# The mean of a first layernorm taken off on TensorE: seven chunks of x are turned, multiplied by a centering matrix and read from PSUM

## The chip, the core and the metric

The kernel runs on one core of one Trainium2 chip. A core has five engines, each with its own queue that is worked in order: TensorE (PE, with its weight loads as PEld), VectorE (DVE), ScalarE (ACT), GpSimd (POOL) and SyncE (SP), and 16 DMA engines that the queues feed. The metric is device time in microseconds (us) of the whole program; lower is better.

## The reference

Two graph-network layers run over 6250 nodes with 64 features and 206250 edges (`src`, `dst`, sorted by `dst`), each behind a layernorm and a relu, and each added to its input:

```python
def _layernorm(x, axis=-1, eps=1e-05):
    m = jnp.mean(x, axis=axis, keepdims=True)
    v = jnp.var(x, axis=axis, keepdims=True)
    return (x - m) / jnp.sqrt(v + eps)
...
h = jnp.maximum(_layernorm(x, axis=-1), 0.0)
x = x + _L0_gnn_ref(h, edge_index, ...)   # twice: h + segment_sum(h[src], dst), then relu(. @ Wa + ba) @ Wb + bb
h = jnp.maximum(_layernorm(x, axis=-1), 0.0)
x = x + _L1_gnn_ref(h, edge_index, ...)   # mlp of messages, segment sum, mlp of both
```

The change is in the first of the two layernorms only, which works on the kernel's input `x`.

## The kernel before

**Layout.** Nodes are cut into NT = 49 tiles of P = 128 nodes. `xs` holds all of x in SBUF, 128 partitions (nodes of a tile) by 49 tiles by D = 64 features. Seven DMAs, four on SP's queue and three on ACT's, bring it in chunks of XT = 7 tiles, the last with its short tile by itself.

**What the program does.** The edge list becomes a dense count matrix A, 6250 by 6250 in bytes, one tile of 128 destination nodes at a time; the segment sums are then products with A on TensorE. The stages are:

1. A prologue. `search` finds where each pair of destination tiles begins in the sorted list, by counting samples of `dst` (ACT, `junk` L312) and then, in `search_block`, entries of a gathered block (`junk` L336). `fetch_blocks` and `fetch_edges` are indirect DMAs issued on POOL (L325, L350) that bring the block and then the edges (`d_win`, `s_win`). `slots`, `cast` and `turn` (DVE, ACT, PE and ACT) make rows `lkw` of indices out of the edges. `values(t)` runs seven times, for the chunks that begin at tile 0, 7, 14, ..., 42: it makes the normed values `h` of seven tiles (`norm`, DVE and ACT) and splits them into three bf16 parts in `hp` (`split`, PE and ACT).
2. A build loop over the 49 tiles. `build(t, ...)` has DVE make one-hot patterns (`there` L414, `high` L418, `low` L421), PE multiply them into counts (`cnt` L446, sixteen at a time), ACT copy the counts (L448), and SP store them to DRAM. Between the quarters of `build(t)`, PE takes the first segment sum of tile t-1 (`acc` L594), which needs `hp` of all 49 tiles.
3. Two sweeps that load A again and take the second and third segment sums (`acc` L771).

**The first layernorm.** `norm` takes the sum over the 64 features (DVE, L239), scales it to a mean (L240), subtracts it (`xm`, L242), squares on ACT (L244), sums the squares (DVE, L246), takes the root on ACT (L247), the reciprocal on DVE (L248), and makes `h` by one DVE instruction that clips at zero and scales (L249). `split` copies `h` to bf16 on ACT (L256), and twice has PE put `h` less the parts so far into PSUM (L259, fp32, two passes each; L261, bf16) and ACT copy the rest to bf16 (L262).

**The order of the work.** A scheduler orders each engine's instructions by their place in the program and by when it takes them to be ready; waits follow from the data and the buffers. `behind(a, b)` fixes the order of two instructions on one engine. The calls ahead of the build loop stand in this order: `search(0)`, `fetch_blocks(0)`, `search(1)`, `fetch_blocks(1)`, `values(0)`, `search_block(0, 0)`, `fetch_edges(0)`, `values(7)`, `slots(0)`, `cast(0)`, `search_block(1, ..)`, `fetch_edges(1)`, `turn(0, 0)`, `values(14)`, `search(2)`, `fetch_blocks(2)`, `values(21)`, `search(3)`, `fetch_blocks(3)`, `values(28)`, `search_block(2, ..)`, `fetch_edges(2)`. `values(35)` and `values(42)` follow the first `build`.

**PSUM.** Eight banks: pool `pacc` has two (the segment sums `acc`), `pmix` two (tag `mix`, through `bank(...)`: the sample product, the turned rows, the layers), and `pcnt` two buffers of two banks, tile `cnt`, which `split` and `build` share. In SBUF `xm` has two buffers for the seven chunks.

In what follows chunk k, for k = 0 to 6, is the one of `values(7 * k)`.

Of the kernel before, what the change touches and what calls it, by code (L numbers as in the profile page):

```python
# [32 lines left out]
FP = mybir.dt.float32  # L33
# [7 lines left out]
OP = mybir.AluOpType  # L41
AX = mybir.AxisListType

P = 128
N = 6250
E = 206250
D = 64
# [6 lines left out]
CH = 512  # L54
# [20 lines left out]
XT = 7  # L75
# [83 lines left out]
def fast(ctx: ExitStack, tc: tile.TileContext, x, src, dst, w, bad, out):  # L159

    nc = tc.nc
# [3 lines left out]
    pacc = ctx.enter_context(tc.tile_pool(name="f_pacc", bufs=2, space=bass.MemoryType.PSUM))  # L165
# [3 lines left out]
    work = building.enter_context(tc.tile_pool(name="f_work", bufs=2))  # L169
    once = building.enter_context(tc.tile_pool(name="f_once", bufs=1))  # L170
# [3 lines left out]
    def bank(name, dtype=FP):  # L174
        return pmix.tile([P, CH * 4 // mybir.dt.size(dtype)], dtype, tag="mix", name=name)
# [7 lines left out]
    xs = const.tile([P, NT, D], FP, name="xs")  # L183
# [18 lines left out]
    nc.gpsimd.iota(high2, pattern=[[1, H], [0, 2]], base=HB, channel_multiplier=0, allow_small_or_imprecise_dtypes=True)  # L202
    which = once.tile([P, NQ], FP, name="which")
    nc.gpsimd.iota(which, pattern=[[P, NQ]], base=0, channel_multiplier=1, allow_small_or_imprecise_dtypes=True)
    ones = const.tile([P, P], FP, name="ones")
    nc.vector.memset(ones, 1.0)
    parts2 = [once.tile([P, MOST, 3, P], BF, name=f"parts{i}") for i in range(2)]
# [9 lines left out]
    ps = bank("ps_smp")  # L217
# [6 lines left out]
    hp = once.tile([P, NT, HP], BF, name="hp")  # L224
# [10 lines left out]
    def norm(to, t, n):  # L235

        xt = xs[:, t:t + n, :]
        mean = work.tile([P, n], FP, name="mean", tag=f"mean{n}")
        begun = nc.vector.tensor_reduce(mean, xt, axis=AX.X, op=OP.add)  # L239
        nc.vector.tensor_scalar_mul(mean, mean, 1.0 / D)  # L240
        xm = work.tile([P, n, D], FP, name="xm", tag=f"xm{n}")
        centered = nc.vector.tensor_tensor(xm, xt, mean[:, :, None].to_broadcast([P, n, D]), op=OP.subtract)  # L242
        sq = work.tile([P, n, D], FP, name="sq", tag=f"sq{n}", bufs=1)
        squared = nc.scalar.activation(sq, xm, AF.Square)  # L244
        var = work.tile([P, n], FP, name="var", tag=f"var{n}")
        nc.vector.tensor_reduce(var, sq, axis=AX.X, op=OP.add)  # L246
        nc.scalar.activation(var, var, AF.Sqrt, bias=w.eps, scale=1.0 / D)  # L247
        nc.vector.reciprocal(var, var)  # L248
        nc.vector.scalar_tensor_tensor(to, xm, 0.0, var[:, :, None].to_broadcast([P, n, D]), op0=OP.max, op1=OP.mult)  # L249
        return begun, centered, squared  # L250

    def split(parts, h):

        parts = [parts[:, :, i * D:(i + 1) * D] for i in range(NP)]
        banks = pcnt.tile([P, 2, CH], FP, name="cnt")[:, :, :h.shape[1] * D]
        nc.scalar.copy(parts[0], h)  # L256
        for i in range(2):
            ps = banks[:, i].rearrange("p (t d) -> p t d", d=D)
            nc.tensor.matmul(ps, w.ident, h, start=True, stop=False)  # L259
            for k in range(i + 1):  # L260
                nc.tensor.matmul(ps, minus, parts[k], start=False, stop=(k == i))  # L261
            nc.scalar.copy(parts[i + 1], ps)  # L262
# [20 lines left out]
    def tiles_of(b):  # L283
        return range(starts[b], starts[b] + BATCHES[b]), slice(starts[b], starts[b] + BATCHES[b])
# [3 lines left out]
    def behind(op, other):  # L288

        tc.add_manual_dep(op.ins, other.ins.name,  # L290
                          mybir.DependencyInfo(mybir.DependencyClass.NoSync, mybir.DependencyReason.DATA),
                          reason="order on an engine")
        return op

    def follow(op, engine):

        if engine in counted:
            behind(op, counted[engine])
# [6 lines left out]
    def search(b, after=None):  # L305

        if b >= len(BATCHES):
            return
        each, qs = tiles_of(b)
        for q in each:  # L310
            junk = wins.tile([P, NB], BF, name="junk", bufs=1)
            op = nc.scalar.activation(junk, smp, AF.Sign, bias=below_node[:, q:q + 1], accum_out=sign1[:, q:q + 1])  # L312
            if after:
                behind(op, after)
            follow(op, "ACT")
        nc.vector.tensor_scalar(row[:, qs], sign1[:, qs], -0.5, NB / 2 - 1, op0=OP.mult, op1=OP.add)
        return op, nc.vector.tensor_scalar(base[:, qs], sign1[:, qs], -0.5 * BLK, (NB / 2 - 1) * BLK + BLK / 2,
                                           op0=OP.mult, op1=OP.add)
# [21 lines left out]
    def fetch_edges(b):  # L340

        if b >= len(BATCHES):
            return
        each, qs = tiles_of(b)
        nc.vector.scalar_tensor_tensor(off_f[:, qs], sign2[:, qs], -0.5, base[:, qs], op0=OP.mult, op1=OP.add)
        nc.vector.tensor_scalar(off[:, qs], off_f[:, qs], float(E - P), None, op0=OP.min)  # L346
        lists[b] = [wins.tile([P, MOST, P], I32, name=name)[:, :len(each), :] for name in ("d_win", "s_win")]
        for win, of in zip(lists[b], (dst, src)):
            for i, q in enumerate(each):
                nc.gpsimd.indirect_dma_start(  # L350
                    out=win[:, i, :], out_offset=None, in_=of.rearrange("(a o) -> a o", o=1),
                    in_offset=bass.IndirectOffsetOnAxis(ap=off[:, q:q + 1], axis=0))
# [3 lines left out]
    def slots(b):  # L356

        if b >= len(BATCHES):
            return
        each, qs = tiles_of(b)  # L360
        n = len(each)
        d, s = lists.pop(b)

        def temp(name, dtype=I32, tag=None):
            return wins.tile([P, MOST, P], dtype, name=name, tag=tag or name, bufs=1)[:, :n, :]

        parts = parts2[b % 2][:, :n]

        def first(op):
            follow(op, "DVE")  # L370

        pair = temp("pair")
        first(nc.vector.tensor_scalar(pair, d, 1, PITCH // 2 - 1, op0=OP.logical_shift_right, op1=OP.bitwise_and))
        pair = pair.bitcast(I16).rearrange("p q (a b) -> p q a b", b=2)
        mine = temp("mine", FP)
        for i, q in enumerate(each):
            nc.vector.tensor_scalar(mine[:, i, :], pair[:, i, :, 0], which[:, q:q + 1], None,
                                    op0=OP.is_equal, op1=OP.add, accum_out=number[:, q:q + 1])
        high = temp("high_i")
        first(nc.vector.tensor_scalar(high, s, 7, 63, op0=OP.logical_shift_right, op1=OP.bitwise_and))  # L380
        nc.vector.scalar_tensor_tensor(parts[:, :, 1, :], mine, float(HB), high, op0=OP.mult, op1=OP.add)
        word = temp("word")
        first(nc.vector.tensor_scalar(word, s, 2, W - 1, op0=OP.logical_shift_right, op1=OP.bitwise_and))
        place = temp("place", tag="high_i")
        first(nc.vector.tensor_scalar(place, s, 3, PLACE_BIT, op0=OP.bitwise_and, op1=OP.logical_shift_left))
        second = temp("second", tag="mine")
        first(nc.vector.tensor_scalar(second, d, 1, SECOND_BIT, op0=OP.bitwise_and, op1=OP.logical_shift_left))
        place, second = (t.bitcast(I16).rearrange("p q (a b) -> p q a b", b=2)[:, :, :, 0] for t in (place, second))
        nc.vector.scalar_tensor_tensor(parts[:, :, 2, :].bitcast(I16), place, ONE_BITS, second,
                                       op0=OP.bitwise_or, op1=OP.bitwise_or)  # L390
        words[b] = word
# [118 lines left out]
        halves(h2r[:, t:t + n], ps[:, :n * HID].rearrange("p (t f) -> p t f", f=HID))  # L510

    def values(t):
        h = work.tile([P, XT, D], FP, name="h")
        begun, centered, squared = norm(h, t, XT)
        if t <= XT:
            behind(begun, sampled)
            behind(begun, bounds)
            behind(squared, searched[0])
        if t == XT:
            behind(centered, searched[1])  # L520
        split(hp[:, t:t + XT], h)


# [26 lines left out]
    searched = search(0)  # L550
    fetch_blocks(0)
    search(1)
    fetch_blocks(1)
    values(0)
    search_block(0, 0)
    fetch_edges(0)
    values(XT)
    slots(0)
    cast(0)
    for i in range(2):  # L560
        op = search_block(1, i)
    fetch_edges(1)
    turn(0, 0)
    values(2 * XT)
    search(2, op)
    fetch_blocks(2)
    values(3 * XT)
# [81 lines left out]
    work = ctx.enter_context(tc.tile_pool(name="f_work2", bufs=2))  # L649
# [14 lines left out]
    ps = bank("ps_stats")  # L664
# [133 lines left out]
    t, n = GROUPS[-1]  # L798
    acc, going = sweep(lambda k: [h2r[:, k, i, :] for i in range(2)], True, 0, conv2, (0, 2, 5, 7, 9, 11), (0, 1, 4, 5, 6, 8), [])
    going.append([conv2(t, n, acc), [0, 2, 10, 14, 17, 20]])  # L800
    acc, _ = sweep(lambda k: [yr[:, k].rearrange("p i d -> p (i d)")], False, 3, conv3, (0, 4, 8, 11), None, going)
# [254 lines left out]
```

## Time and profile before

| what | value |
|---|---|
| median of 5 runs | 878.99 us (878.92 to 880.21) |
| profiled execution, device time | 878.99 us |
| its span, first to last instruction | 877.1 us |
| mean granted TensorE clock | 0.993 |
| busy, share of the span | PE 96%, PEld 83%, DVE 73%, ACT 64%, POOL 16% |
| L239, L242, L246, L249 (DVE, 128x448 f32), seven each | 620, 614, 609, 617 ns (medians) |
| L244 (ACT, 128x448 f32), seven | 561 ns (median) |
| moved by DMA | 133.58 MB |

The device time is the span and 1.9 us around it. The profile is one execution, taken by the hardware profiler. Busy time is counted by engine, and instructions of one engine may overlap a little, so a sum of durations can pass the time that they took. A wait is put down to whichever releaser came last by the profile. PEclk is the share of TensorE's full clock that was granted.

### The profile page before, as it was taken

Reading aid. Unit: us, or ns where it says so; the run is one execution under the profiler, and the core shown is the slowest. Engines: PE = TensorE matmul, PEld = TensorE weight load, DVE = VectorE, ACT = ScalarE, POOL = GpSimd, SP = SyncE. Lnnn points to the kernel's source line nnn. Section 1 sums busy time; section 2 is a strip of 40 time slices with the busy share of each in tenths; the row PEclk is TensorE's granted clock in tenths of the full one; section 3 lists DMA queues with packets and bytes.
Section 4 is the critical chain, followed back from the end, with each engine's and each line's share of the span. In section 5 each row is a group of like instructions: output and inputs, shape, how many; then the busy total and the mean of one; then the engine's idle time right before and its main releaser. Section 6 shows DMA issues by size and latency. Waiting matters only on the chain.

```text
span 877.1 us, 19654 instructions
## 1 busy us (share of the span) xinstructions
PE 844.0 (96%) x8178; PEld 724.3 (83%) x8178; DVE 637.3 (73%) x957; ACT 565.6 (64%) x761; POOL 137.3 (16%) x86
## 2 busy tenths in 40 slices
PE   3789999999999999999999999999999999999996
PEld 1479999999999999887888787888889887777785
DVE  5899999999999999645555555555456677767662
ACT  5767777677777666645555555555555689877763
POOL 3545654435432300000000000000000000000000
PEclk9899999999999999999999999999999999999998
DMA  6345555556544434634443444444434477777771
GB/s 148 103 123 159 175 147 152 153 150 176 158 144 143 140 112 142 213 112 132 127 123 123 125 121 124 124 121 123 133 93 133 152 250 247 231 238 226 233 215 49
DMA packets 148327, 133.58 MB, mean 152 GB/s; under 512 B 29988, under 2 KB 110500, under 8 KB 148228
## 3 DMA queue, kind: packets, MB, share of 16 engines
q1 hardware_dynamic: 141784, 121.19, 46.3%
q0 software_dynamic: 3600, 10.32, 4.2%
q8 instruction: 66, 1.08, 0.5%
q10 hardware_dynamic: 2844, 0.72, 0.4%
q14 instruction: 33, 0.27, 0.1%
HBM read 91.25 MB, written 40.94 MB: 151 GB/s over the span
## 4 chain that ended last, share of the span: by engine, by line
PE 85%; ACT 6%; DMA 4%; DVE 3%; issue 1%; SPq 0%; POOL 0%; ACTq 0%; DVEq 0%
PE acc L771 44%; PE acc L594 21%; PE cnt L446 8%; PE ps_t L459 6%; PE ps_y L468 3%; ACT ar L762 2%; DMA a<-A 2%; ACT a L448 1%; PE ps_g L509 1%; ACT t L461 1%; ACT junk L312 1%; DMA blk<-in_dst_dram,row 1%; DMA xs<-in_x_dram 1%; PE cnt L259 1%; DMA s_win<-in_src_dram,off 0%
## 5 line engine op out<-in xcount | busy, mean ns | idle before, releaser
L762 DVE CAST ar<-a 128x2048 fp32r<-128x2048 uint8 (+1 forms) x200 | 220.3, 1110 | 175.4 <-PE acc L771 153.5
L762 ACT CAST ar<-a 128x2048 fp32r<-128x2048 uint8 (+2 forms) x126 | 232.1, 1846 | 117.1 <-PE acc L771 101.7
L771 PE MATMUL acc<-ar,h2r 128*128 128x512 f32 (+2 forms) x1274 | 297.1, 387 | 0.0
L771 PEld LDWEIGHTS acc<-ar,h2r 128*128 128x128 f32 x1274 | 228.8, 189 | 49.8 <-issue 5.8
L594 PE MATMUL acc<-hp,a 128*128 128x193 bf16 x2352 | 232.1, 247 | 1.4 <-ACT a L448 0.6
L448 ACT ACTIVATE a<-cnt 128x784 int16<-128x784 f32 x196 | 161.0, 822 | 69.6 <-PE cnt L446 68.7
L594 PEld LDWEIGHTS <-a 128*128 128x128 fp8e4 x2352 | 191.6, 97 | 3.4 <-ACT a L448 2.4
L771 PE MATMUL acc<-ar,yr 128*128 128x512 f32 (+2 forms) x637 | 156.9, 398 | 0.0
L771 PEld LDWEIGHTS acc<-ar,yr 128*128 128x128 f32 x637 | 115.5, 189 | 32.5 <-issue 9.4
L446 PEld LDWEIGHTS <-low 128*128 128x128 fp8e4 x3136 | 107.4, 96 | 8.9 <-issue 8.4
L446 PE MATMUL cnt<-high,low 128*128 128x49 bf16 x3136 | 114.0, 186 | 0.5 <-ACT a L448 0.3
L421 DVE TENSOR_TENSOR low<-there,lkw 128x2048 int32<-128x2048 bf16 (+2 forms) x51 | 112.2, 2200 | 0.0
L418 DVE TENSOR_TENSOR high<-high,lkw 128x3136 bf16<-128x3136 bf16 (+2 forms) x51 | 87.8, 1721 | 5.2 <-PE cnt L446 5.2
L325 POOL DMA_INDIRECT blk<-in_dst_dram,row x25 | 57.6, 2303 | 87.5 <-DVE own L590 74.4
L414 DVE TENSOR_TENSOR there<-word,lkw 128x2048 bf16<-128x2048 bf16 (+2 forms) x51 | 59.1, 1176 | 0.4
L350 POOL DMA_INDIRECT s_win<-in_src_dram,off x25 | 46.1, 1843 | 7.6 <-issue 7.6
L350 POOL DMA_INDIRECT d_win<-in_dst_dram,off x25 | 31.4, 1257 | 61.9 <-DVE off L346 46.2
L259 PE MATMUL cnt<-h,ident 128*128 128x448 f32 x28 | 17.7, 735 | 13.0 <-DVE h L249 10.3
L461 ACT ACTIVATE t<-ps_t,d 128x512 f32<-128x512 f32 (+2 forms) x26 | 17.3, 664 | 11.6 <-PE ps_t L459 11.6
L461 ACT ACTIVATE t<-ps_t,c 128x512 f32<-128x512 f32 (+1 forms) x26 | 17.1, 662 | 11.3 <-PE ps_t L459 11.3
L259 PEld LDWEIGHTS cnt<-h,ident 128*128 128x128 f32 x28 | 5.4, 233 | 19.9 <-issue 9.0
L336 ACT ACTIVATE junk<-blk,below_node 128x550 bf16<-128x550 int32 x25 | 18.7, 749 | 3.3 <-DMA blk<-in_dst_dram,row 3.3
(123 smaller groups left out, 606.1 us busy)
## 6 DMA issues: line engine op xcount, KB each, us to landing
a<-A SPq DMA_DIRECT2D x276, 256.0 KB, 2.8
A<-a SPq DMA_DIRECT2D x49, 768.0 KB, 4.1
a<-A SPq DMA_DIRECT2D x24, 192.0 KB, 2.4
a<-A SPq DMA_DIRECT2D x22, 64.0 KB, 2.0
out_dram<-o SPq DMA_DIRECT2D x11, 128.0 KB, 2.9
A<-a SPq DMA_DIRECT2D x49, 16.0 KB, 4.7
xs<-in_x_dram ACTq DMA_DIRECT2D x3, 224.0 KB
xs<-in_x_dram SPq DMA_DIRECT2D x3, 224.0 KB, 6.9
```

Of the source, the lines that this page charges most:

```text
L325: nc.gpsimd.indirect_dma_start(out=blks[q], out_offset=None, in_=dst.rearrange("(r b) -> r b", b=BLK), in_offset=bass.IndirectOffsetOnAxis ...
L350: nc.gpsimd.indirect_dma_start(out=win[:, i, :], out_offset=None, in_=of.rearrange("(a o) -> a o", o=1), in_offset=bass.IndirectOffsetOnAx ...
L414: nc.vector.tensor_tensor(there, word2[:, None, :, :].to_broadcast(shape), of(0)[:, :, None, :].to_broadcast(shape), op=OP.is_equal)
L418: nc.vector.tensor_tensor(high, high2[:, None, :, :].to_broadcast(shape), of(1)[:, :, None, :].to_broadcast(shape), op=OP.is_equal)
L421: counted["DVE"] = nc.vector.tensor_tensor(low.rearrange("p (g i) w -> p g i w", i=2), there.rearrange("p g w i -> p g i w"), of(2)[:, :, ...
L446: counted["PE"] = nc.tensor.matmul(ps[:, b, j * H:(j + 1) * H], low[:, g, :], high[:, g // 2, :, g % 2], start=True, stop=True)
L448: counted["ACT"] = nc.scalar.activation(a[:, :, k:k + 2 * PG].rearrange("p h (b j) -> p h b j", b=2), ps[:, :, :PG * H].rearrange("p b (j ...
L459: placed(nc.tensor.matmul(ps[:, :n * P], wt, rhs, start=(i == 0), stop=(i == len(terms) - 1)))
L461: nc.scalar.activation(to, ps[:, :n * P], AF.Relu, bias=bias)
L594: nc.tensor.matmul(acc[:, t % 2, :], self.own if k == t else self.a[:, k, :], hp[:, k], start=(k == order[0]), stop=(k == t))
L762: widen(ar.rearrange(f"p k t b -> {order}"), a.rearrange(f"p t (k b) -> {order}", b=P))
L771: op = nc.tensor.matmul(acc[:, :cols], part, ar[:, k - k0].rearrange("p t b -> p (t b)")[:, :cols], start=first, stop=(k == H - 1 and i == ...
```

## The change

The sum, its scaling and the subtraction leave VectorE for the first layernorm. In their place, for each chunk of seven tiles, TensorE turns pairs of tiles (128 nodes by 2 x 64 features, to 128 features by 128 nodes) into a PSUM bank, four of them, the last pair overlapping the third by one tile. The bank is copied to SBUF, by VectorE for chunks 0 and 1 and by ScalarE for the other five. TensorE then multiplies each turned pair by `center`, a 128 x 128 matrix of two 64 x 64 blocks with the identity less 1/64 on each, which gives the nodes' rows back with their mean taken off, in a PSUM bank of the pool `pacc`. ScalarE's square and VectorE's last instruction read them there. The rest of `norm` becomes `scaled`, which both layernorms use; the second layernorm keeps the mean on VectorE. The norm of chunk 2 is called ahead of `slots(0)`, while its `split` stays where it was. The fixed orders change with it.

```diff
+    center = once.tile([P, P], FP, name="center")
+    nc.gpsimd.memset(center, 0.0)
+    for j in range(0, P, D):
+        nc.gpsimd.memset(center[j:j + D, j:j + D], -1.0 / D)
+    nc.vector.tensor_tensor(center, center, w.ident, op=OP.add)
...
-        centered = nc.vector.tensor_tensor(xm, xt, mean[:, :, None].to_broadcast([P, n, D]), op=OP.subtract)
+        nc.vector.tensor_tensor(xm, xt, mean[:, :, None].to_broadcast([P, n, D]), op=OP.subtract)
+        scaled(to, xm, n)
+
+    def scaled(to, xm, n):
...
     def values(t):
+
+        ps = bank("xt")
+        sides = [(min(j, XT - 2), j - min(j, XT - 2)) for j in range(0, XT, 2)]
+        for i, (j, _) in enumerate(sides):
+            nc.tensor.transpose(ps[:, i * P:(i + 1) * P], xs[:, t + j:t + j + 2, :].rearrange("p t d -> p (t d)"), w.ident)
+        xt = work.tile([P, CH], FP, name="xt", tag="t1")
+        begun = (nc.vector.tensor_copy if t <= XT else nc.scalar.copy)(xt, ps)
+        xm = pacc.tile([P, CH], FP, name="acc")
+        for i, (j, o) in enumerate(sides):
+            nc.tensor.matmul(xm[:, (j + o) * D:(j + 2) * D], xt[:, i * P:(i + 1) * P], center[:, o * D:], start=True, stop=True)
         h = work.tile([P, XT, D], FP, name="h")
-        begun, centered, squared = norm(h, t, XT)
+        squared = scaled(h, xm[:, :XT * D].rearrange("p (t d) -> p t d", d=D), XT)
         if t <= XT:
             behind(begun, sampled)
             behind(begun, bounds)
-            behind(squared, searched[0])
-        if t == XT:
-            behind(centered, searched[1])
+        else:
+            behind(begun, searched[0])
+        behind(squared, searched[0])
+        if t == 2 * XT:
+            return h
         split(hp[:, t:t + XT], h)
...
     values(XT)
+    h = values(2 * XT)
     slots(0)
...
     turn(0, 0)
-    values(2 * XT)
+    split(hp[:, 2 * XT:3 * XT], h)
     search(2, op)
```

More of the change, by code (lines that the diff above doesn't have):

```diff
@@ L238, in norm @@
         mean = work.tile([P, n], FP, name="mean", tag=f"mean{n}")
-        begun = nc.vector.tensor_reduce(mean, xt, axis=AX.X, op=OP.add)
+        nc.vector.tensor_reduce(mean, xt, axis=AX.X, op=OP.add)
         nc.vector.tensor_scalar_mul(mean, mean, 1.0 / D)
         xm = work.tile([P, n, D], FP, name="xm", tag=f"xm{n}")
-        centered = nc.vector.tensor_tensor(xm, xt, mean[:, :, None].to_broadcast([P, n, D]), op=OP.subtract)
+        nc.vector.tensor_tensor(xm, xt, mean[:, :, None].to_broadcast([P, n, D]), op=OP.subtract)
+        scaled(to, xm, n)
+    def scaled(to, xm, n):
         sq = work.tile([P, n, D], FP, name="sq", tag=f"sq{n}", bufs=1)
@@ L249, in norm @@
         nc.vector.scalar_tensor_tensor(to, xm, 0.0, var[:, :, None].to_broadcast([P, n, D]), op0=OP.max, op1=OP.mult)
-        return begun, centered, squared
+        return squared
     def split(parts, h):
```

## The prediction

> **What bounds the kernel now.** I read the page's slices first (tenths busy in 40 slices of 21.9 us):
>
> ```profile
> PE   3789999999999999999999999999999999999996
> ...
> DVE  5899999999999999645555555555456677767662
> ACT  5767777677777666645555555555555689877763
> ...
> PEclk9899999999999999999999999999999999999998
> ```
>
> PE is full from the fourth slice to the last but one, and only the first three show room. The change touches nothing after them, so it can win or lose only there. Next, busy time by stretch (PE, PEld, DVE, ACT, POOL, then clock, DMA share, GB/s):
>
> ```profile
> 17.00:27.00 10.00, 8.29 (x21) 3.07 (x21) 8.03 (x29) 9.06 (x26) 5.99 (x7) 1.00 0.25 63
> 27.00:37.00 10.00, 7.13 (x31) 3.02 (x29) 8.41 (x26) 6.12 (x14) 6.78 (x7) 0.74 0.43 133
> 47.00:57.00 10.00, 6.97 (x111) 4.97 (x109) 9.79 (x22) 5.84 (x11) 8.23 (x6) 1.00 0.18 52
> ...
> 100.00:150.00 50.00, 49.77 (x904) 48.18 (x902) 49.38 (x72) 36.59 (x66) 29.53 (x14) 1.00 0.57 167
> ```
>
> By 100 us PE lacks 0.23 us in 50. So the end moves by as much as PE reaches that state sooner or later, at about 56 us. Ahead of it nobody is full throughout: ACT comes nearest in 17 to 27, DVE in 47 to 57. Which wait ends last is read in the timeline (start, duration, engine, line, then idle time before it and its releaser):
>
> ```profile
> 26.94 0.68 DVE L421 TENSOR_TENSOR low<-there,lkw 128x512 int32<-128x512 bf16 x1
> ...
> 30.17 0.75 ACT L336 ACTIVATE junk<-blk,below_node 128x550 bf16<-128x550 int32 x1 [1.33 <-DMA blk<-in_dst_dram,row]
> ...
> 30.92 0.28 ACT L247 ACTIVATE var<-var,eps 128x7 f32<-128x7 f32 x1
> 31.24 0.20 DVE L248 RECIPROCAL var<-var 128x7 f32<-128x7 f32 x1 [1.03 <-ACT var L247]
> ...
> 32.30 1.86 PE L259 MATMUL cnt<-h,ident 128*128 128x448 f32 x2 [2.00 <-DVE h L249]
> ...
> 34.33 0.87 PE L446 MATMUL cnt<-high,low 128*128 128x49 bf16 x16
> ...
> 37.87 0.61 DVE L242 TENSOR_TENSOR xm<-xs,mean 128x448 f32<-128x448 f32 x1
> ...
> 39.51 0.20 DVE L248 RECIPROCAL var<-var 128x7 f32<-128x7 f32 x1 [1.04 <-ACT var L247]
> ...
> 49.73 0.99 PE L259 MATMUL cnt<-h,ident 128*128 128x448 f32 x2 [2.53 <-DVE h L249]
> ```
>
> The patterns for the first counts are there at 27.62, yet the counts start at 34.33: PE stands at the split of chunk 4, whose root sat on ACT behind a `junk` that waited for a gathered block. From 26.13 (first pattern) to 51.79 (`low` of tile 2) DVE idles only 1.03, 0.34, 0.21 and 1.04 us, 2.6 in all: it carries the path there, with PE's splits and ACT's roots between. At 47.2 PE waits 2.53 us for chunk 6's `h`.
>
> **The change, part by part.** Prices come from these rows (groups: busy us, mean ns; timeline: the next line's start gives the occupancy):
>
> ```profile
> L267 DVE TENSOR_TENSOR h2r<-ps_g,h2r 128x512 fp32r<-128x512 f32 x12 | 8.3, 691 | 2.9 <-ACT h2r L266 2.6
> L266 ACT CAST h2r<-ps_g 128x512 fp32r<-128x512 f32 x12 | 7.0, 585 | 2.1 <-PE ps_g L509 0.9
> ```
> ```profile
> 82.59 0.38 PE L484 MATMUL tf<-ident,r 128*128 128x128 f32 x2
> 82.81 0.58 PE L446 MATMUL cnt<-high,low 128*128 128x49 bf16 x16
> ...
> 133.15 1.06 PE L509 MATMUL ps_g<-w,t 128*128 128x128 f32 x8
> 134.04 0.58 PE L446 MATMUL cnt<-high,low 128*128 128x49 bf16 x16
> ```
>
> *VectorE.* Gone: seven L239 at 0.620 and seven L242 at 0.614, 8.6 us, and seven L240, which showed 0.04 to 0.20 each, about 0.5. New: two copies out of PSUM, at most 0.691 each (L267 reads a second operand too), 1.4 us. Net 7.7 us less. Most of that lies before 25 us, where DVE also waits for gathers: of the L239, L240 and L242 only the `xm` at 37.87 comes after 26.3.
>
> *ScalarE.* Five copies of 0.585 (L266, same shape) to 0.69 (L461, 512 wide), 2.9 to 3.4 us; I take 2.9. The square reads PSUM instead of SBUF: nothing (0.561 now; L262 reads 448 from PSUM in 0.537). In 27 to 57 ACT has 9.6 us idle or waiting, which hides the copies there. In 17 to 27 only 0.94 is free. A copy is also a wait put into ACT's queue: behind it stand the search's `junk`, the roots and the casts of `hp`, and for them wait POOL's gathers and PE.
>
> *TensorE.* Per chunk four transposes (0.22 for two, so 0.44) and four fp32 products in eight passes (0.89): 1.33 us, 9.3 for seven, at full clock. At the slow one L259 shows 0.93 against 0.51 a pass, so up to 2.4 a chunk. PE now idles 4.8 us between 8.68 and 13.46, which hides chunks 0 and 1, and again 2.0 before 32.30 and 4.2 from there to 56. Work on chunks 5 and 6 falls into that end at 2.7 us, and only what is left of the idle time pays for it. A chunk's `xm` comes 0.44 + 0.16 fill + 0.69 + 0.89 + 0.17 fill = 2.35 us after PE begins, against 1.9 from 7.87 to 9.76 now. No one waits for chunk 0 that early.
>
> *New buffer waits.* `xm` takes the two banks that the first segment sum uses. The first `acc` then needs chunk 5's `h` done; that ended at 41.34 and the first L594 began at 41.27, so the wait costs nothing unless chunk 5 falls back. The turned rows share two banks with the sample product and with `turn`: a late copy would hold up `turn(0, 0)` (24.48) behind it on PE.
>
> *The rest.* `center` costs POOL three memsets and DVE one 128x128 add (the casts L193 took 0.22), in POOL's idle time from 2.8 to 10.95 and DVE's from 1.1 to 5.76: nothing; without that cover, under 1 us. The earlier norm of chunk 2 moves DVE and ACT work ahead of `slots(0)`, past no DMA of its own.
>
> [...] PE ran at a granted 0.50 in 32 to 38 us after 2.0 us of idle; the two L259 pairs there took 1.86 each against 1.02 at 44.00. Filling PE's gaps should hold the clock: two pairs at 0.84, three L261 at 0.22, and 48 counts (0.75) come to 3.1 us. [...] I leave the 3.1 out of my sum and use it for the lower end.
>
> **The sum.** (1) The `xm` at 37.87 leaves DVE's path: 0.6. (2) The two waits for a root, 1.03 and 1.04, shrink if chunks 4 and 5 are normed earlier. Chunk 4's `xm` was made at 23.31, 0.95 after its buffer came free, so DVE held it; but its square then stood on ACT until 26.97, so ACT held it longer. Bounds 0 and 2.1; I take the middle, 1.0. (3) Ahead of 26.13, DVE's queue held the chain in three places: `row` at 10.52 behind a mean at 9.79 though ACT was done at 9.92 (0.5), an `h` inside `slots(0)` at 21.82 (0.5), and `there` behind an `xm` at 25.59 (0.55). Bounds 0 and 1.55; I take 1.0, since a PE turnaround now stands in some of these places. Together 2.6, so 878.99 - 2.6 = **876.4 us**. The profiled execution, at 878.99, is also the median, so no shift is needed. All three at their upper bounds give 4.2 (874.8). PE's own bound is 2.0 + 4.2 + 3.1 - 2.7 = 6.6 us (872.4), if DVE's patterns move earlier too.
>
> **Rivals.** *Slower: ScalarE's queue.* The copies of chunks 2, 3 and 4 fall into the stretch where ACT had 0.94 us free. Each takes 0.585 and may stand for its transposes, which sit on PE behind one pair of L259 (1.0): 3 x 1.59 - 0.94 = 3.8 us later for chunk 4's root, hence for 32.30 and everything after, less 0.6 for step 1: +3.2, 882.2 us. It decides once copies and their waits add over 0.94 us there without time coming back in the 3.9 us that ACT idles in 27 to 37. For it: 9.06 of 10, and chunk 4's square that already waited there. Against: ACT idles 4.1 us in 7 to 17, where the first of these copies may go. *No change: POOL and the gathers.* Edge gathers are issued one after the other from 21.15, the block's at 26.67, its data at 30.17, and only then `junk` and the root. If that order stays, 7.7 us of DVE buy step 1 alone: 878.4. For it: POOL shows gaps of only 0.30 between those issues. Against: the first of them waited for DVE and ACT. *The work is only moved:* chunk 6's `h` still comes after `low`, and PE pays 2.7 us for chunks 5 and 6 against step 1: 881.1.
>
> **Chances.** A measurement of this kernel can tell 0.2%, 1.76 us, from no change. Forecast (over that faster) 0.47; gathers, or gains and losses that cancel, 0.20; ScalarE's queue 0.23 and moved work 0.10, 0.33 slower. The range goes from PE's bound, 872.4, to just past ScalarE's price, 882.8, leaving about 0.06 below and 0.12 above. The two signs together hold most of the chance: the forecast's own range is 872.4 to 877.2.
>
> **What would show it.** Right: DVE's busy time falls from 637.3 by about 7.7 and ACT's rises by about 3; the first L446 starts before 33, chunk 6's `h` before 47, and the first unbroken row of L594 and L446 (56.17 now) comes 2 to 4 us earlier; PEclk stays at 1.00 in 32 to 38. Wrong: that row comes no earlier, with ACT's new copy as the releaser of a wait or with PE waiting for the turned rows; the sample product (7.06) or `row` (10.52) starts later because transposes took PE first; or the loop after 60 us changes its pace.

## The result, and the profile after

The changed kernel takes 895.4 us (median of ten executions, 889.74 to 896.93) against 879.9 us of the kernel before, run next to it: a ratio of 1.0164 [1.0144, 1.0184], slower (this ratio, like those below, compares all the runs and not the two medians). The prediction said 876.4 us, in 872.4 to 882.8. The profiled execution is the fastest of the ten: 889.74 us, span 887.9, which is 10.8 over the span before.

Line numbers shift with the diff: the norm's sum of squares L246, root L247, reciprocal L248 and `h` L249 are now L255 to L258, the splits L259 and L261 are L268 and L270, the search's `junk` L336 is L345, the patterns L414, L418, L421 are L423, L427, L430, the counts L446 are L455, the first segment sum L594 is L616. New are L526 (turning x), L528 (the copies), L531 (the products).

The page's slices, as before in tenths of 22 us:

```profile
PE   5589999999999999999999999999999999999996
...
DVE  4589999999999999545554545554556676767662
ACT  5577777777776666555555555555545588877773
...
PEclk9899999999999999999999999999999999999999
```

PE is busier in the first slice (5 for 3) and emptier in the second (5 for 7). From the fourth slice on it is as full as before: the loss lies in the same three slices where the prediction looked for a gain. Busy time by stretch (PE, PEld, DVE, ACT, POOL, then clock, DMA share, GB/s):

```profile
17.00:27.00 10.00, 8.47 (x43) 4.82 (x42) 4.98 (x20) 8.60 (x24) 5.37 (x6) 1.00 0.24 52
27.00:37.00 10.00, 2.87 (x9) 1.61 (x8) 7.92 (x25) 4.21 (x11) 5.89 (x7) 0.68 0.42 127
...
47.00:57.00 10.00, 6.86 (x33) 4.21 (x33) 9.45 (x22) 7.84 (x19) 3.27 (x2) 0.96 0.32 87
100.00:150.00 50.00, 49.77 (x902) 48.17 (x899) 49.75 (x71) 36.04 (x62) 31.26 (x12) 1.00 0.57 164
```

In 17 to 27 VectorE fell from 8.03 to 4.98 and nothing came to fill it. In 27 to 37 PE has 2.87 of 10 (7.13 before): there it stands still. In 47 to 57 it is as busy as before, with 33 matmuls for 111, because the many short segment sums are missing. The loop's own row is unchanged. The timeline gives the reason (start, duration, engine, line, then idle time before it and its releaser):

```profile
23.07 0.43 DVE L423 TENSOR_TENSOR there<-word,lkw 128x512 bf16<-128x512 bf16 x1 [0.84 <-ACT lkw L414]
...
25.18 0.58 ACT L528 COPY xt<-xt 128x512 f32<-128x512 f32 x1
...
25.99 1.45 PE L531 MATMUL acc<-center,xt 128*128 128x128 f32 x12
...
28.92 0.29 DVE L389 TENSOR_SCALAR high_i<-s_win 128x256 int32<-128x256 int32 x1 [3.48 <-DMA s_win<-in_src_dram,off]
...
30.00 0.75 ACT L345 ACTIVATE junk<-blk,below_node 128x550 bf16<-128x550 int32 x1 [4.24 <-DMA blk<-in_dst_dram,row]
...
31.17 0.54 ACT L253 ACTIVATE sq<-acc 128x448 f32<-128x448 f32 x1
...
31.96 0.60 DVE L255 TENSOR_REDUCE var<-sq 128x7 f32<-128x448 f32 x1
...
34.56 1.86 PE L268 MATMUL cnt<-h,ident 128*128 128x448 f32 x2 [7.13 <-DVE h L258]
...
39.73 0.52 PE L455 MATMUL cnt<-high,low 128*128 128x49 bf16 x14 [0.43 <-ACT hp L271]
...
45.47 0.83 ACT L457 ACTIVATE a<-cnt 128x784 int16<-128x784 f32 x1
...
45.92 1.92 PE L526 MATMUL xt<-ident,xs 128*128 128x128 f32 x8
...
52.37 0.61 DVE L258 SCALAR_TENSOR_TENSOR h<-acc,var 128x448 f32<-128x448 f32 x1
...
53.03 1.02 PE L268 MATMUL cnt<-h,ident 128*128 128x448 f32 x2 [3.05 <-DVE h L258]
...
57.78 1.27 PE L616 MATMUL acc<-hp,a 128*128 128x193 bf16 x13
```

The same places in the kernel before, chunk 3's square first:

```profile
20.17 0.56 ACT L244 ACTIVATE sq<-xm 128x448 f32<-128x448 f32 x1
...
26.13 0.42 DVE L414 TENSOR_TENSOR there<-word,lkw 128x512 bf16<-128x512 bf16 x1
...
40.38 0.83 ACT L448 ACTIVATE a<-cnt 128x784 int16<-128x784 f32 x1
...
41.27 0.51 PE L594 MATMUL acc<-hp,a 128*128 128x193 bf16 x4 [0.38 <-ACT a L448]
41.62 0.94 PE L259 MATMUL cnt<-h,ident 128*128 128x448 f32 x2
...
45.25 1.96 PE L594 MATMUL acc<-hp,a 128*128 128x193 bf16 x21
```

The first pattern starts at 23.07 instead of 26.13: the gain ahead of it came, 3.06 us of it. Then it is lost, in two places.

*Chunks 3 and 4.* PE has their centered values ready by 27.44. ACT's next instruction after the copy is not their square but the third search's `junk`, which waits 4.24 us for its block; the square follows at 31.17 (chunk 3's stood at 20.17 before). VectorE meanwhile waits 3.48 us for `s_win`, with the sum of squares queued behind it at 31.96. PE, 7.13 us without work, starts the split of chunk 3 at 34.56 at a granted clock of 0.50, and the first counts start at 39.73 for 34.33.

*Chunks 5 and 6.* Their turning starts at 45.92 and their splits at 53.03; before, the two splits stood at 41.62 and 49.73. The first segment sum shares `pacc`'s two banks with their `xm`. It starts at 57.78 instead of 41.27. Before, 41 of its 49 products were worked off between 41.27 and 47.2, in PE's time between the splits; now none. The 16.5 us have three parts in the trace. The first tile's counts are copied by 46.30 instead of 41.21, which is the loss of chunks 3 and 4 handed on (5.0). Chunk 5's `h` is read out of the shared bank by 52.98 (6.7). Then the splits of both chunks and sixteen counts stand ahead on PE (4.8).

In the trace the loop runs at a constant 7.6 us of delay from tile 4 to tile 48. Another 1.5 us go at the start of the first sweep, and 1.6 after the 750th of the sweeps' 1911 products. That last stretch was 1.9 to 6.8 us longer than in the trace of before in every other trace too, whatever the kernel, so I read the traces at the loop and at product 750.

### The profile page after: what moved, and what is told of

The parts are those of the page before. It is cut to its first block, busy times and chain, and to the rows that moved or that the text cites. A ratio compares the mean times of both kernels' runs of the same rounds, so it can differ in the third digit from the quotient of the medians.

```text
span 887.9 us, 19820 instructions
## 1 busy us (share of the span) xinstructions
PE 852.0 (96%) x8262; PEld 733.4 (83%) x8262; DVE 630.6 (71%) x939; ACT 569.5 (64%) x766; POOL 135.7 (15%) x89
## 4 chain that ended last, share of the span: by engine, by line
PE 88%; ACT 5%; DMA 3%; DVE 2%; issue 1%; POOL 0%; SPq 0%; DVEq 0%; ACTq 0%; POOLq 0%
PE acc L793 45%; PE acc L616 21%; PE cnt L455 8%; PE ps_t L468 6%; PE ps_y L477 4%; DMA a<-A 2%; ACT a L457 1%; PE ps_g L518 1%; ACT junk L321 1%; PE cnt L268 1%; ACT t L470 1%; ACT ar L784 1%; DMA s_win<-in_src_dram,off 1%; DMA smp_i<-in_dst_dram 1%; DMA blk<-in_dst_dram,row 0%
## 5 line engine op out<-in xcount | busy, mean ns | idle before, releaser
L616 PE MATMUL acc<-hp,a 128*128 128x193 bf16 x2352 | 231.8, 247 | 0.8
L616 PEld LDWEIGHTS <-a 128*128 128x128 fp8e4 x2352 | 191.5, 97 | 1.8 <-ACT a L457 1.6
L455 PE MATMUL cnt<-high,low 128*128 128x49 bf16 x3136 | 113.6, 186 | 2.1 <-DVE low L430 1.1
L455 PEld LDWEIGHTS <-low 128*128 128x128 fp8e4 x3136 | 106.9, 96 | 9.2 <-issue 7.4
L430 DVE TENSOR_TENSOR low<-there,lkw 128x2048 int32<-128x2048 bf16 (+2 forms) x51 | 112.2, 2199 | 0.0
L427 DVE TENSOR_TENSOR high<-high,lkw 128x3136 bf16<-128x3136 bf16 (+2 forms) x51 | 87.8, 1722 | 12.8 <-PE cnt L455 12.6
L423 DVE TENSOR_TENSOR there<-word,lkw 128x2048 bf16<-128x2048 bf16 (+2 forms) x51 | 59.1, 1176 | 1.4 <-ACT lkw L414 1.1
L268 PE MATMUL cnt<-h,ident 128*128 128x448 f32 x28 | 14.6, 619 | 13.5 <-DVE h L258 12.1
L345 ACT ACTIVATE junk<-blk,below_node 128x550 bf16<-128x550 int32 x25 | 18.7, 746 | 5.2 <-DMA blk<-in_dst_dram,row 5.2
L470 ACT ACTIVATE t<-ps_t,e 128x512 f32<-128x512 f32 (+2 forms) x28 | 17.5, 630 | 3.2 <-PE ps_t L468 3.2
```

Source lines behind the costliest of these rows:

```text
L423: nc.vector.tensor_tensor(there, word2[:, None, :, :].to_broadcast(shape), of(0)[:, :, None, :].to_broadcast(shape), op=OP.is_equal)
L427: nc.vector.tensor_tensor(high, high2[:, None, :, :].to_broadcast(shape), of(1)[:, :, None, :].to_broadcast(shape), op=OP.is_equal)
L430: counted["DVE"] = nc.vector.tensor_tensor(low.rearrange("p (g i) w -> p g i w", i=2), there.rearrange("p g w i -> p g i w"), of(2)[:, :, ...
L455: counted["PE"] = nc.tensor.matmul(ps[:, b, j * H:(j + 1) * H], low[:, g, :], high[:, g // 2, :, g % 2], start=True, stop=True)
L470: nc.scalar.activation(to, ps[:, :n * P], AF.Relu, bias=bias)
L616: nc.tensor.matmul(acc[:, t % 2, :], self.own if k == t else self.a[:, k, :], hp[:, k], start=(k == order[0]), stop=(k == t))
```

## The experiments

Theory A: the order is the loss. The norms' steps stand in ACT's and VectorE's queues behind instructions that wait for gathers, and chunks 5 and 6 hold the segment sum's banks. Theory B: the added work on PE and ACT is the loss. Theory C: `center` and the changed layout are.

Each set of runs shares one chip with the kernel before, which took 891.1 us in the first set, 891.6 in the second, 881.3 in the third; so times are compared as ratios. For traces of the first two sets I take the landmarks of `before_center` (below) as the reference, since its loop has their pace. This table holds the differences in us, each from its reference's trace (third set and the first row: the trace of before). The two references themselves differ by 0.5, 0.6 and 0.3 us at the first three landmarks, so a half us there says nothing:

| kernel | ratio | first counts | second tile's | first segment sum | loop, tile 24 | sweeps, product 750 |
|---|---|---|---|---|---|---|
| changed, first trace | 1.0164 | +5.4 | +6.6 | +16.5 | +7.6 | +9.1 |
| after_again | 1.0150 | +7.0 | +10.6 | +21.5 | +10.7 | +12.3 |
| after_order | 1.0130 | +6.5 | +9.2 | +20.1 | +9.8 | +11.3 |
| t012 | 1.0098 | +6.3 | +5.1 | +5.3 | +5.9 | +5.9 |
| t01234 | 1.0088 | +11.2 | +5.9 | +13.6 | +7.7 | +8.7 |
| early34 | 1.0085 | -2.9 | +4.5 | +15.4 | +5.5 | +7.0 |
| early56 | 1.0081 | +8.2 | +3.2 | +9.4 | +5.0 | +6.6 |
| early_all | 1.0001 | -2.9 | -3.1 | +4.1 | +0.4 | +1.4 |
| before_early | 1.0000 | +1.0 | -1.1 | +5.7 | +0.8 | +0.8 |
| t012b | 0.9992 | +0.1 | -3.2 | -0.8 | -2.1 | -2.0 |
| t012e56 | 0.9979 | -0.7 | -4.1 | +2.7 | -2.3 | -2.3 |
| before_order | 0.9977 | -2.3 | -1.1 | -2.6 | 0.0 | -0.1 |

**before_center**: the kernel before with `center` built and never read.

```diff
+    center = once.tile([P, P], FP, name="center")
+    nc.gpsimd.memset(center, 0.0)
+    for j in range(0, P, D):
+        nc.gpsimd.memset(center[j:j + D, j:j + D], -1.0 / D)
+    nc.vector.tensor_tensor(center, center, w.ident, op=OP.add)
```

> The kernel before with only the matrix center built in its place, read by nobody. Theory C, layout: the 512 bytes a partition shift what lies behind them in SBUF, and the first loads of the sweep wait for another tile, so that the sweep starts later; then 1 to 2 us slower, with the prologue unmoved. Otherwise no change, within 0.5 us.

Measured: 890.49 us, ratio 0.9992 [0.9978, 1.0006]. Theory C falls as far as `center` goes, and the prediction's "nothing" for it holds; early_all, below, has the rest of the changed layout.

**t012 and t01234**: the change for chunks 0 to 2, or 0 to 4, alone; the later chunks keep the mean on VectorE.

```diff
     def values(t):
+        if t // XT not in (0, 1, 2):      # t01234: (0, 1, 2, 3, 4)
+            h = work.tile([P, XT, D], FP, name="h")
+            norm(h, t, XT)
...
+            split(hp[:, t:t + XT], h)
+            return
```

> Chunks 0, 1 and 2 turned as in the change, chunks 3 to 6 with the mean on VectorE as before; the order of calls is the changed one. Theory A, queues: the loss came because the turned chunks 3 and 4 reached ScalarE only behind a junk that waited 4.2 us for a gathered block, and because chunks 5 and 6 hold the two banks that the first segment sum needs. Then the first counts start at 31 to 34 us instead of 39.7, the first segment sum near 41 instead of 57.8, and the time is 875 to 880, no slower than before. Theory B, work: the added products and copies cost by themselves wherever they stand. Then three sevenths of the loss of 14 us stay: about 885.

> Chunks 0 to 4 turned, chunks 5 and 6 with the mean on VectorE as before. Theory A: chunks 3 and 4 are held as in the changed kernel (first counts at 39 to 40 us), but the first segment sum no longer waits for chunk 5's bank and starts near 46, so 2 to 4 us of the loss come back. Theory B: two sevenths of 14 us come back, 4 us, and the first counts move by as much as the two chunks' work, 2.7 us, only if that stood ahead of them, which it did not.

Measured: 898.8 us, 1.0098 [1.0070, 1.0126], and 898.84 us, 1.0088 [1.0064, 1.0111]. The first counts come at 40.07 and 45.03, in both later than Theory A expected. Theory B's price by the chunk, 6 and 10 us over the kernel before, stands against 7.7 and 7.8. But neither is to be read as a price of chunks, because the edit let go of something else. In the kernel before, the means of chunks 0 and 1 had fixed orders behind the sample; the means that are left have none, and in t012 two of them went to the front of VectorE's queue, ahead of the sample `smp_d` on which the whole search rests. VectorE in t012:

```profile
9.73 0.62 DVE L244 TENSOR_REDUCE mean<-xs 128x7 f32<-128x448 f32 x1 [2.75 <-DMA xs<-in_x_dram]
...
11.69 0.54 DVE L220 TENSOR_TENSOR smp_d<-ident,smp_f 125x375 f32<-125x375 f32 x1
```

A mean that waits 2.75 us for its part of x holds `smp_d` (6.46 before), and the first counts come 6.3 us late. In t01234, where the means of chunks 5 and 6 are left without an order, `smp_d` is on time, since PE starts on it at 5.76 (7.06 before), but PE then waits 4.36 us for `base`, which goes with the first search's `row`, until 13.45 (`base` stood at 10.58 in the trace of before). In t012 it is again an instruction that waits for a DMA at the head of VectorE's queue; for t01234 that is my reading of the late `base`. t012b, below, mends t012.

**after_order**: the changed kernel with the third search's `junk` forced behind the root of chunk 4 on ACT, so that no norm waits behind it there.

```diff
-        nc.scalar.activation(var, var, AF.Sqrt, bias=w.eps, scale=1.0 / D)
+        roots.append(nc.scalar.activation(var, var, AF.Sqrt, bias=w.eps, scale=1.0 / D))
...
-        search_block(2, i)
+        behind(search_block(2, i), roots[4])
```

> The changed kernel with one order fixed: on ScalarE the two junk of the third search stand behind chunk 4's root. Nothing is added or taken away. Theory A: chunk 3's square runs at 26.5 to 27 instead of 31.2, the first counts come 3 to 4 us sooner (36), and the time falls by about as much. Theory B: no change, within 1 us.

Measured: 902.57 us, 1.0130 [1.0099, 1.0161], within the uncertainty of the changed kernel itself. The 3 to 4 us did not come. ACT and VectorE show where they stayed:

```profile
26.71 0.55 ACT L255 ACTIVATE sq<-acc 128x448 f32<-128x448 f32 x1
...
29.35 0.29 DVE L391 TENSOR_SCALAR high_i<-s_win 128x256 int32<-128x256 int32 x1 [3.96 <-DMA s_win<-in_src_dram,off]
...
32.06 0.61 DVE L257 TENSOR_REDUCE var<-sq 128x7 f32<-128x448 f32 x1
...
32.70 0.30 ACT L258 ACTIVATE var<-var,eps 128x7 f32<-128x7 f32 x1 [5.45 <-DVE var L257]
```

The square moved from 31.17 to 26.71, and the sum of squares stayed at 32.06, behind `high_i`. The norm was held in two queues at once; freeing one changes nothing that can be measured.

**after_again, early34, early_all**: the changed kernel itself, and two versions that change no work, only the places of the calls (and, so that the norms can stand early, the number of `h`'s buffers). early34 takes the norms of chunks 3 and 4 ahead of `slots(0)`, where the change had put that of chunk 2; early_all also takes those of chunks 5 and 6 ahead of the first `build`. The splits stay where they were.

```diff
# early34 (and `if 2 * XT <= t <= 4 * XT: return h`, three buffers of h)
-    h = values(2 * XT)
+    hs = [values(k * XT) for k in range(2, 5)]
     slots(0)
...
-    values(3 * XT)
+    split(hp[:, 3 * XT:4 * XT], hs[1])
...
-    values(4 * XT)
+    split(hp[:, 4 * XT:5 * XT], hs[2])
# early_all besides (and `if t >= 2 * XT: return h`, four buffers of h)
+    hs += [values(5 * XT), values(6 * XT)]
...
-                values(5 * XT)
+                split(hp[:, 5 * XT:6 * XT], hs[3])
...
-                values(6 * XT)
+                split(hp[:, 6 * XT:7 * XT], hs[4])
```

> The changed kernel once more, on the chip and beside the kernel before that the other runs of this set share, since the level of a run differs by some 12 us from chip to chip. Every theory: 10 to 15 us slower than before, first counts 5 to 6 us and the loop's steady state 7 to 8 us later.

> The changed kernel with the norms of chunks 3 and 4 called ahead of slots(0) too, as chunk 2's is (three buffers for h); their splits stay where they were. Nothing is added or taken away. Theory A, refined after the first set (on PE the transposes of chunk 3 follow turn(0, 0), and so chunks 3 and 4 are queued on ScalarE and VectorE behind work that waits for the gathers of the second batch): first counts at 30 to 34 us instead of 39.7, and 4 to 6 us of the loss come back; what chunks 5 and 6 cost, 2 to 3 us, stays. Theory B, work: no change within 1 us.

> As early34, and the norms of chunks 5 and 6 called ahead of the first build (four buffers for h), their splits behind it as they were. All of the added work is still done. Theory A: the first segment sum finds its bank free and starts at 36 to 41 instead of 57.8; steady state no later than before, and the time from 3 us faster to 1 us slower than before. Theory B: still 10 us slower or more.

Measured: 905.27 us, 1.0150 [1.0128, 1.0172]; 899.25 us, 1.0085 [1.0063, 1.0108]; 892.12 us, 1.0001 [0.9987, 1.0016]. early_all does every transpose, copy and product of the change and costs nothing that can be measured. So Theory B falls, and the order makes the whole loss. Some landmarks missed what was expected: after_again's first counts are 7.0 and its loop 10.7 us late, and early_all's first segment sum starts at 45.01, not by 41. PE in early34:

```profile
30.89 0.53 PE L455 MATMUL cnt<-high,low 128*128 128x49 bf16 x14 [0.43 <-issue]
...
50.20 1.86 PE L268 MATMUL cnt<-h,ident 128*128 128x448 f32 x2 [4.02 <-DVE h L258]
...
56.34 1.27 PE L616 MATMUL acc<-hp,a 128*128 128x193 bf16 x13
```

The first counts come at 30.89, 2.9 us *before* those of the reference: for this step the prediction's reading of the prologue was right, once the norms stand early. The lead is then lost to chunks 5 and 6, whose split still starts at 50.20 and behind which the segment sum waits until 56.34; what is left of the loss, 7.6 us in the median, is more than the 2 to 3 expected. In early_all that sum starts at 45.01 and fills PE's gaps again:

```profile
39.34 1.51 PE L455 MATMUL cnt<-high,low 128*128 128x49 bf16 x32 [4.89 <-DVE low L430]
...
45.01 1.26 PE L617 MATMUL acc<-hp,a 128*128 128x193 bf16 x7
46.11 0.94 PE L268 MATMUL cnt<-h,ident 128*128 128x448 f32 x2
...
55.43 0.24 PE L455 MATMUL cnt<-high,low 128*128 128x49 bf16 x3 [0.44 <-issue]
57.08 1.58 PE L617 MATMUL acc<-hp,a 128*128 128x193 bf16 x13 [1.41 <-ACT a L457]
```

Within the first tile PE still waits 4.89 us for `low`, whose engine, VectorE, had waited 2.56 us for `s_win` at 30.67 and worked without a gap since. The second tile's counts nevertheless start 3.1 us early. That lead goes in the third tile, most of it in the two gaps of PE at 55.43 and 57.08, so that the fourth starts 0.6 us early.

**early56**: only the second half of that, chunks 5 and 6.

```diff
-        if t == 2 * XT:
+        if t in (2 * XT, 5 * XT, 6 * XT):
             return h
...
     values(4 * XT)
+    hs = [values(5 * XT), values(6 * XT)]
```

> The changed kernel with only the norms of chunks 5 and 6 called ahead of the first build; the norms of chunks 3 and 4 stay where the change has them. Theory A (order in the queues and banks): the part of the loss that early34 left, 7.8 us at the end, belongs to these two chunks, and what the early norms of 3 and 4 gave back, 4 to 5 us, stays lost here. So the first count stays about 7 us late, the first segment sum comes far sooner than the 21.5 us late of the changed kernel (under 14 late), and the time is 3 to 8 us over the kernel before, ratio 1.003 to 1.009. Theory B (added work on PE and ACT): the same work, so the same time as the changed kernel, ratio 1.014 to 1.017.

Measured: 888.41 us, 1.0081 [1.0061, 1.0101]. The first counts are 8.2 us late, and yet half of the loss is gone. The first segment sum starts at 50.67, between the splits again:

```profile
49.18 1.70 PE L268 MATMUL cnt<-h,ident 128*128 128x448 f32 x2
50.67 1.27 PE L617 MATMUL acc<-hp,a 128*128 128x193 bf16 x7
```

The two places add up. Early norms of 3 and 4 give 1.0150 - 1.0085 = 0.0065, those of 5 and 6 give 1.0150 - 1.0081 = 0.0069, together 0.0134; both at once gave 0.0149, each step uncertain by some 0.003.

**before_early**: the kernel before, mean on VectorE, with the calls placed as in early_all.

> The kernel before, with its mean on VectorE, and only the calls moved as in early_all: norms of chunks 2 to 4 ahead of slots(0), of 5 and 6 ahead of the first build. It tells what early_all owes to its order and what to the change. If the means on VectorE then stand in the way of the gathers, as the prediction held, the first count comes later than in the kernel before (by 1 to 4 us) and the time is over it, ratio 1.001 to 1.005, so that the change is worth 1 to 4 us in that order. If VectorE's time is free there, first count and time are as in early_all or better: ratio 0.996 to 1.000, and the change is worth nothing in any order.

Measured: 882.02 us, 1.0000 [0.9985, 1.0015]. Both answers were half right. The first counts come 1.0 us later than before and 3.9 later than in early_all, so VectorE's means do stand in the way there. The ratio is the same as early_all's all the same: the 3.9 us at the first tile are worth nothing by tile 24, so in this order the change is worth nothing that can be measured.

**t012b and t012e56**: chunks 0 to 2 turned, the means of chunks 3 to 6 on VectorE but behind the first search (t012b); in t012e56 the norms of chunks 5 and 6 also go ahead of the first `build`.

```diff
# t012b: as t012, and in norm
-        nc.vector.tensor_reduce(mean, xt, axis=AX.X, op=OP.add)
+        begun = nc.vector.tensor_reduce(mean, xt, axis=AX.X, op=OP.add)
+        if n == XT:
+            behind(begun, searched[1])
# t012e56: besides, after values(4 * XT)
+    hs = [values(5 * XT), values(6 * XT)]
```

> Chunks 0 to 2 turned, 3 to 6 with the mean on VectorE; as t012, but no mean on VectorE may pass the first search's row and base, which in t012 were 5 us late behind means that waited for x. Theory A: first counts no later than 34 and the time within 2 us of before. Theory B: three sevenths of the loss, 4 to 6 us slower.

> A version meant to beat both: chunks 0 to 2 turned, means of 3 to 6 on VectorE behind the first search (t012b), and the norms of 5 and 6 called ahead of the first build. The old norms hold no segment-sum bank, so they can go early at no price to PE. Theory A: the 2.0 us that t012b was ahead in the loop stay or grow by up to 1.5, ratio 0.995 to 0.999. If VectorE's patterns for tiles 0 and 1 wait behind the four moved instructions, 1 to 3 us are lost instead, ratio 1.000 to 1.003.

Measured: 891.42 us, 0.9992 [0.9977, 1.0007], and 879.79 us, 0.9979 [0.9962, 0.9996]. Where the chunks that come late keep an `xm` in SBUF, they hold no bank of the segment sum. t012e56 leads by 3.5 us at tile 4 and by 2.3 at tile 24, and is faster than both kernels by a margin that its interval just resolves. How much of that the three turned chunks give and how much the moved calls no run separates; before_order, below, has the same ratio by an order alone. Compare busy time by stretch with that of the change:

```profile
27.00:37.00 10.00, 7.22 (x50) 3.46 (x50) 9.99 (x32) 9.76 (x25) 5.00 (x6) 1.00 0.38 116
...
47.00:57.00 10.00, 10.00 (x203) 10.00 (x200) 9.51 (x21) 6.85 (x11) 7.46 (x6) 1.00 0.46 140
```

VectorE and ACT are full in 27 to 37, PE in 47 to 57.

**before_order**: the kernel before with after_order's rule, nothing else.

> The kernel before with the two counts of the third search (junk of search_block(2, .)) forced behind the root of chunk 4 on ACT, nothing else. The prediction read that chunk 4's root waited on ACT for this junk and so held PE's first counts. Theory A: the first count comes 1 to 2.5 us sooner, the block's edges for the third pair as much later; time 0 to 2 us under the kernel before, ratio 0.998 to 1.000. If the third pair's gathers carry the path there, it is 1 to 3 us slower, ratio 1.001 to 1.003.

Measured: 879.43 us, 0.9977 [0.9960, 0.9994]. The first counts come 2.3 us sooner, as the prediction's reading of 32.30 (a root behind a waiting `junk`) says. In the trace none of it is left from the third tile on. The time is nevertheless lower, and the clock may be why: over twelve executions its median is 0.9945, beside 0.992 of the kernel before. That is a correlation; no run set the clock by itself. The trace does not show it: 27 to 37 is granted in full (0.74 before), but 37 to 47 and 47 to 57 have 0.83 each (0.92 and 1.00 before).

```profile
27.00:37.00 10.00, 7.71 (x82) 4.05 (x80) 10.00 (x29) 8.61 (x21) 5.76 (x4) 1.00 0.37 113
37.00:47.00 10.00, 7.93 (x56) 5.43 (x52) 9.04 (x15) 6.96 (x17) 8.12 (x5) 0.83 0.40 115
47.00:57.00 10.00, 8.19 (x109) 5.73 (x110) 8.59 (x20) 5.99 (x11) 6.10 (x4) 0.83 0.26 77
```

## Why the prediction was wrong

**The prices were near.** VectorE's busy time fell by 6.7 us (forecast 7.7), ACT's rose by 3.9 (2.9), PE's by 8.0 (9.3). The copies, by their minimum, median and maximum in ns:

```profile
L528 ACT COPY xt<-xt x5: 574/577/587, 13.2 to 48.3; 128x512 f32<-128x512 f32 x5
L528 DVE COPY xt<-xt x2: 690/691/692, 9.4 to 10.2; 128x512 f32<-128x512 f32 x2
```

The prediction took 585 and 691, so the prices of the copies were right. Step (3) of its sum, 1.0 with bounds 0 to 1.55, was too small if anything: the first `there` came 3.06 us sooner.

**The step that failed is (2).** It said that the waits for a root "shrink if chunks 4 and 5 are normed earlier", a gain of 1.0 with bounds 0 and 2.1. Instead chunks 3 and 4 were normed later: chunk 3's square by 11.0 us (31.17 for 20.17), PE's wait in front of a split grew from 2.00 to 7.13, and the first counts came 5.4 late. Its reason, that VectorE held chunk 4's `xm`, says when work may start; what decides is where it stands in the queues. Between the old `xm` and the square there was no wait on PE; now there is, and the scheduler put the third search's `junk` and the second batch's `high_i` ahead. Both wait for gathers that the change hardly moves: blocks issued one after the other from 26.34 (26.67 before), `s_win` from 23.76 (23.65). The bound below should have been a loss: chunk 3's square had stood at 20.17, and its place behind the block's arrival was about 31, up to 11 us later. Freed VectorE time (3.05 us in 17 to 27) then had nothing to do, because the work that could have filled it stood behind the waits.

**The buffer wait was seen and priced at nothing.** That "the wait costs nothing unless chunk 5 falls back" was the right condition. Chunk 5 did fall back, from a split at 41.62 to 53.03, and the condition had no price: the first segment sum started 16.5 us later, 5.0 of them because its counts were late. early56 gives half of the loss back by calling these two norms earlier. That frees the bank and moves the splits at once, and no run separates the two: the changed kernel with its `xm` in other banks was not tried. The prediction charged chunks 5 and 6 with 2.7 us of work on PE; the 41 products that had run there from 41.27 to 47.2 and now came later stood in no term.

**The rivals.** "ScalarE's queue" had the right engine, the right sign and 882.2 us. Its mechanism was occupancy: copies that take 0.585 each in a stretch with 0.94 free. The copies did not fill it: ACT's busy time in 17 to 27 fell from 9.06 to 8.60. The `junk` waiting 4.24 us held ACT after that, and after_order shows that ACT alone does not carry the loss. "The work is only moved" named chunks 5 and 6, priced at their 2.7 us of PE work instead of at what waits for their bank. "No change: the gathers" named the gathers that hold both queues.

**The clock went the other way.** The prediction kept 3.1 us of clock gain for the lower end, an estimate from one stretch of the kernel before, 0.50 in 32 to 38 behind 2.00 us of idle. No run shows that filled gaps alone would bring it. In the trace 27 to 37 was granted 0.68 (0.74 before), with 7.13 us without PE work in it. From one execution to the next the chunk 5 and 6 splits differ as well: after_again shows

```profile
54.73 1.86 PE L268 MATMUL cnt<-h,ident 128*128 128x448 f32 x2 [3.21 <-DVE h L258]
...
56.77 1.70 PE L268 MATMUL cnt<-h,ident 128*128 128x448 f32 x2
```

where the changed kernel's first trace has 1.02 and 0.91 after a gap of 3.05 us. Clock granted: 0.50 in 54.7 to 60 there, 1.00 in 53 to 58 here. Over the ten executions of the changed kernel the mean clock goes from 0.992 (889.74 us) to 0.984 (896.93), 0.9 us for each 0.001, so most of what the median lost beyond the profiled execution goes with the clock. What decides between such outcomes no run shows. The gaps of 3.05 and 3.21 us had opposite ones, and in the kernel before the 2.00 us ahead of 32.30 were followed by 0.50 and the 2.53 us ahead of 49.73 by 1.00.

**Still open.** The delay grows from 7.6 to 9.1 us where the first sweep begins and loads A; no run took this apart. Nor did one show why the kernel before itself took 879 to 892 us from set to set: from tile 4 to tile 48 it is 282.2 us in its first trace, and 290.2 in before_center's, 0.18 us for each tile. The chip alone need not be the reason: the record gives the second and the third set the same chip number, and the kernel before took 891.6 and 881.3 us there.

## What to carry to other kernels

Where work is moved to another engine, the price is not only its duration: look at which instruction will stand ahead of it in *each* queue that it passes, and whether that one waits for a DMA. Here a new buffer in the banks of a later stage made that stage wait 6.7 us for the new work, so price such a wait beside the work's own time. When a change has its promised busy times and is slower, move the calls and leave the work: here that gave all of 1.5% back.

## What was not expected of the hardware

- The eight transposes of chunks 5 and 6 took 1.92 us at 45.92; those of chunks 3 and 4 took 1.20 (0.93 and 0.27) at 23.00 and 23.96. The granted clock was 0.50 from 44.33 to 47.75, although from 40.00 to 44.30 PE had worked 2.67 us of 4.30, with no gap over 1.06; in the kernel before it was 1.00 from 49.73 to 56.00, behind a gap of 2.53.
- The mean granted clock goes with a spread of 6 us between executions of one kernel: the kernel before in the third set has 877.86 us at 0.998 and 883.71 at 0.988.
